# Attention of the second layer: two tiles of the second sequence's probabilities turned by squares instead of on TensorE, its bias added by GpSimd, and maxima ahead of value sums

## The chip, the cores and the metric

The kernel runs on one core of a Trainium2 chip. The core has five instruction queues that run beside each other and meet through semaphores: TensorE (PE: matmuls and 128x128 transposes, from SBUF into PSUM), VectorE (DVE), ScalarE (ACT), GpSimd (POOL) and SyncE (SP, which here only issues transfers). Transfers (DMAs) that SP, ACT and POOL issue are carried out by 16 DMA engines. The metric is the time of one execution on the device in microseconds; smaller is better. The kernel before takes 454.44 us (median of 3 runs, 454.12 to 454.5).

## The reference, cut to what matters

Two sequences (b = 0, 1) of 512 rows with 512 numbers, in float32, go through two layers: an attention with a memory matrix and a feed-forward net with ternary weights, then a plain attention and a feed-forward net, a layer norm after each of the four. The change is in the third of these, the plain attention with one head of 128:

```
qkv = einsum('bsc,cf->bsf', x, Wqkv) + bqkv          # 512 -> 3 x 128
q, k, v = qkv[:, :, 0], qkv[:, :, 1], qkv[:, :, 2]   # after a reshape
attn = softmax(einsum('bqd,bkd->bqk', q, k) / sqrt(128))
out = einsum('bqk,bkd->bqd', attn, v)
x = layernorm(x + einsum('bqd,dc->bqc', out, Wo) + bo)
```

After it comes `x = layernorm(x + (silu(x @ Wg.T) * (x @ Wu.T)) @ Wd.T)`, which is where the kernel spends its last 180 us.

## The kernel before, in words

All names below are of the kernel; line numbers are those of the profile. P is 128, a tile is 128 rows of 512 numbers, NT = 4 tiles make a sequence (t = 0 to 3), NK = 4 blocks of 128 columns make a row, TURNED = 2, SQ = 32.

**Order of the work.** The program is written in one order; a scheduler puts the instructions of each engine in a fixed order of its own, except on POOL, whose order is that of the text. `tc.issue_after(x.ins)` tells it that what follows in the block comes after x. An engine runs its queue strictly in order, so an instruction that waits holds up all behind it. PSUM has eight banks of 128x512, handed out by `psum(name)`; who takes a bank waits until the last reader of what stood in it is done.

**Turning a matrix.** A matmul contracts over partitions, so rows have to be transposed. The kernel does it in two ways. (1) TensorE transposes blocks of 128x128 into PSUM with the identity, and ScalarE or VectorE copies the result to SBUF: `transposed` (L118 to L131) does so for a whole sequence, block by block, four transposes from four tiles and a copy per block. (2) By squares: VectorE's `transpose` turns each 32x32 square of a tile where it stands (L1195), and `move_squares` (L301) moves the 4x4 kinds of squares to their places by transfers of 32 partitions each; `queues=3` gives SP eight of them, POOL four, and VectorE copies the four on the diagonal (L320); `queues=2` gives SP eight and POOL eight; `queues=1` gives SP twelve, with the diagonal.

**The stage.** For each sequence b (loop at L1147), TensorE makes q and k (`pqk`, L1163; ScalarE adds their bias, L1169) and v for each tile (`pv`, L1181), and VectorE adds the bias of v, reading PSUM (L1187). Sequence 0 then goes on at once: `scores` (L1110) makes four tiles of q k (`psc`, L1117), each in its own bank; `maxima` (L1120) takes the largest of each row on VectorE (L1123) and scales it (L1124); `exponentials` (L1129) lets ScalarE write the probabilities and their sums (L1139). The probabilities of sequence 0 are turned by squares (L1195 and, in the second pass of the loop, `move_squares(squares, pt0)`), while GpSimd adds the output bias bo to its rows (L1196). In between, `split_up` prepares the next feed-forward weights: ScalarE takes the upper part of a weight (L1033), VectorE forms two remainders (L1043 reads a part and the weight, L1044 two parts; all in SBUF).

For sequence 1: four score tiles, four maxima, four exponentials, then a table load on ScalarE for the later Silu (L1096). A small copy on POOL, `landed` (L1209), waits until the squares of sequence 0 have landed; behind it POOL issues four transfers that add bo from memory to the rows of sequence 1 (L1211). `split_up(2)` follows the maxima.

Then the ends of both sequences, in TensorE's order: `values(0, pt0, 1)` (L1228: probabilities times v, four matmuls into one bank, copied to `ot` by ScalarE, L1233), the 16 transposes of the probabilities of sequence 1 (`transposed`, L128, two copies on VectorE and two on ScalarE, L130), the four output products of sequence 0 (`output`, L1245), `values(1, pt1, 2)` in two halves of the query rows (tiles 0 and 1, then 2 and 3; each half copied to `ot` by VectorE), three output products of sequence 1, 16 transposes of the finished rows of sequence 0 for the feed-forward net (`turn_rows`, L1295), the fourth output product, and the feed-forward products (L1398, L1353). Beside it, `attended` (L1250) adds a product, divided by the sum of the exponentials, to the rows on VectorE; `norm_a1` takes statistics on VectorE (L138, L140), three short steps on POOL (L146, L147, L1240) and the norm itself on ScalarE (L1241).

Of the kernel before, what the change touches and what calls it, by code (L numbers as in the profile page):

```python
# [10 lines left out]
F32 = mybir.dt.float32  # L11
# [8 lines left out]
P = 128  # L20
# [10 lines left out]
SQ = 32  # L31
# [8 lines left out]
def kernel(  # L40
# [285 lines left out]
    def pair_tile(name, dtype=F32):  # L326
        return wop.tile([P, 2, HID], dtype, tag="wo", name=name)
# [764 lines left out]
    def table(func, behind):  # L1092

        with tc.issue_after(behind.ins):
            warm = small.tile([1, 1], F32, tag="warm", name=f"warm_{func.name}", bufs=1)
            nc.scalar.activation(warm, ln_eps[0:1], func)  # L1096
# [29 lines left out]

        return got, maxima

    def exponentials(b, got, behind={}):  # L1129
        sums = small.tile([P, NT], F32, tag="sums", name=f"sums_{b}")  # L1130
        row = []
        for t, (p, mx) in enumerate(got):
            if t % 2 == 0:
                two = pair_tile(f"prob_{b}_{t}")
            e = two[:, t % 2, :]
            with ExitStack() as tied:
                if t in behind:
                    tied.enter_context(tc.issue_after(behind[t].ins))
                moved = nc.scalar.activation(  # L1139
                    e, p, AF.Exp, bias=mx, scale=scale, accum_out=sums[:, t : t + 1]  # L1140
                )
            row.append(e)
        probs.append((row, sums))
        return moved

    qkv = []
    for b in range(B):  # L1147
        if b:
            with tc.issue_after(copies[-2].ins), tc.issue_after(copies[-1].ins):
                split_up(0, room0)  # L1150
                split_up(1, room1[:6])
        qk = []
        qk2 = query_tile(f"qk_{b}")
        if b == 0:
            v2 = query_tile("v")
        pqk = [psum(f"pqk_{b}_{j}") for j in range(2)]
        xt = [xt_a11[:, :TURNED], xt_a11[:, TURNED:]] if b else xt_a10
        for half in (1, 0) if b else (0, 1):
            for j in range(2):
                for k in range(NK):  # L1160
                    p = pqk[j].rearrange("p (h t i) -> p h t i", h=2, i=P)[:, half]
                    rows = xt[half][:, :, k, :]
                    nc.tensor.matmul(  # L1163
                        p, wqkv[:, k, ts(j, D)], rows,
                        start=(k == 0), stop=(k == NK - 1),
                    )
        for j, p in enumerate(pqk):
            s = qk2[:, j, :]
            moved = nc.scalar.activation(s, p, AF.Identity, bias=bqk[:, j : j + 1])  # L1169
            qk.append(s)  # L1170
        if b:
            pt0 = fp.tile([P, NT, NK, P], F32, tag="it10", name="pt_p0", bufs=1)
            move_squares(squares, pt0)
            pt0 = pt0.rearrange("p t k i -> p k t i")
        else:
            table(AF.Exp, moved)
        v = v2[:, b, :].rearrange("p (t d) -> p t d", t=NT)
        for t in range(NT):
            p = psum(f"pv_{b}_{t}")
            for k in range(NK):  # L1180
                nc.tensor.matmul(  # L1181
                    p[:, :D],
                    xt[t // TURNED][:, t % TURNED, k, :],
                    wqkv[:, k, ts(2, D)],
                    start=(k == 0), stop=(k == NK - 1),
                )
            nc.vector.tensor_add(v[:, t, :], bv, p[:, :D])  # L1187
        qkv.append((qk[0], qk[1], v))
        if b == 0:
            got, maxima = scores(0, turn_others)  # L1190
            maxima(range(NT))
            exponentials(0, got)
            squares = fp.tile([P, NT, HID], F32, tag="it00", name="squares_p0", bufs=1)
            for t in range(NT):
                nc.vector.transpose(squares[:, t, :], probs[0][0][t])  # L1195
                nc.gpsimd.tensor_add(xs[0][t], xs[0][t], bo)  # L1196
# [5 lines left out]
            weight_upper(gus[turn[2]][:, a].rearrange("p k i -> p (k i)"), room2[3 * a])  # L1202

    got, maxima = scores(1)
    scaled_max = maxima(range(NT))
    table(AF.Silu, exponentials(1, got))

    landed = small.tile([P, 1], F32, tag="off", name="landed")
    nc.gpsimd.tensor_copy(landed[2 * SQ : 3 * SQ], pt0[2 * SQ : 3 * SQ, NK - 1, NT - 1, P - 1 :])  # L1209
    for t in range(NT):  # L1210
        nc.gpsimd.dma_start(xs[1][t], bo_in.to_broadcast([P, HID]), accum_op=ALU.add)  # L1211
    with tc.issue_after(scaled_max.ins):
        done = split_up(2, room2, True)
    with tc.issue_after(done.ins):
# [6 lines left out]
    def values(b, pt, cuts):  # L1221

        ot = ot2[:, b, :]
        w = S // cuts
        for i in range(cuts):
            po = psum(f"pot_{b}_{i}")
            for k in range(NT):
                nc.tensor.matmul(  # L1228
                    po[:, :w].rearrange("p (t i) -> p t i", i=P), qkv[b][2][:, k, :],
                    pt[:, k, ts(i, NT // cuts)],  # L1230
                    start=(k == 0), stop=(k == NT - 1),
                )
            (nc.vector.tensor_copy if b else nc.scalar.copy)(ot[:, ts(i, w)], po[:, :w])  # L1233
        ots.append(ot)
# [8 lines left out]
    def output(b, t):  # L1243
        p = psum(f"po1_{b}_{t}")
        nc.tensor.matmul(p, ots[b][:, ts(t, P)], wo1, start=True, stop=True)  # L1245
        return p

    def attended(b, t, p):
        x = xs[b][t]
        return nc.vector.scalar_tensor_tensor(  # L1250
            x, p, probs[b][1][:, t : t + 1], x, ALU.mult, ALU.add
        )
# [46 lines left out]
        return pts, turned  # L1299

    values(0, pt0, 1)
    pt1 = transposed(probs[1][0], "p1").rearrange("p k (t i) -> p k t i", t=NT)
    for t in range(NT):
        attended(0, t, output(0, t))
        norm_a1(0, t)
    values(1, pt1, 2)
    for t in range(NT - 1):
        done = attended(1, t, output(1, t))
    rooms = [rows_room(0, "r0"), None]
    x3 = [row_blocks(rooms[0]), None]  # L1310
    pts, turned = turn_rows(0)
    with tc.issue_after(turned.ins):
        p = output(1, NT - 1)
    in_turn = Chain(done)
    for pt, (h, m, _) in zip(pts, x3[0]):
        in_turn(lambda: upper_lower(pt, h, m)[1])
    for t in range(NT - 1):
        in_turn(lambda: norm_a1(1, t))
    in_turn(lambda: attended(1, NT - 1, p))
    x = xs[1][NT - 1]  # L1320
    stats = layernorm_stats(x, f"a11_{NT - 1}")
    in_turn.last = taken[f"a11_{NT - 1}"]
    squares = xtp.tile([P, NT, HID], F32, tag="xt", name="squares_r1")
    for t in range(NT - 1):
        in_turn(lambda: nc.vector.transpose(squares[:, t, :], xs[1][t]))
    in_turn(lambda: layernorm_apply(x, x, stats))
    in_turn(lambda: nc.vector.transpose(squares[:, NT - 1, :], x))
    for h, m, d in x3[0]:
        in_turn(lambda: crossed(d, h, m))
    xt_r1 = fp.tile([P, NT, NK, P], F32, tag="it10", name="xt_f11", bufs=1)  # L1330
# [233 lines left out]
    for i, (b, j) in enumerate(steps):  # L1564
        held.append(up1(b, j, held))
        finished = held[0][0]
        if i == AHEAD:
            with tc.issue_after(in_turn.last.ins), tc.issue_after(uppers.ins):
                moved = finish_up()
        elif i > 1:  # L1570
            while len(held) > 1:
                moved = finish_up()
        if i == 1:
            in_turn(lambda: split_up(AHEAD - 1, take(6)))
        elif i == 2:
            rooms[1] = rows_room(1, "r1")
            x3[1] = row_blocks(rooms[1])
            for k in range(NK):
                with tc.issue_after(in_turn.last.ins):
                    uppers, in_turn.last = rows_from_squares(k)  # L1580

            landed = small.tile([P, 1], F32, tag="off", name="landed_r1")
            nc.gpsimd.tensor_copy(landed[:SQ], x3[1][NK - 1][0][:SQ, S - 1 :].bitcast(F32))
            gus[2:6] = up_weights(gu1_in, "1", range(2, 6), nc.gpsimd)
            wds = down_weights(wd1_in, "1", nc.gpsimd)
        elif i == AHEAD:
            for h, m, d in x3[1]:
                in_turn(lambda: crossed(d, h, m))
        with tc.issue_after(moved.ins):
            if ahead <= last and finished == 1:  # L1590
                split_up(
                    ahead, room0 if ahead == AHEAD else take(6 if turn[ahead] < last else 4)
                )
                ahead += 1
            for _ in range(2):
                if len(down_parts) <= last and len(free) >= (15 if ahead <= AHEAD + 3 else 9 if ahead <= last else 3):
                    split_down()
        if (b, j) == (1, last - 1):
            quarters = [split_tile(0, 0)]

        if i == last:

            with tc.issue_after(moved.ins):
                nc.gpsimd.drain()
# [69 lines left out]
```

## Time and profile before

| | |
|---|---|
| median of 3 runs | 454.44 us (454.12 to 454.5) |
| the profiled execution | 453.49 us, of which the span from the first to the last instruction is 451.7 us |
| mean granted clock of TensorE | 0.997 of full speed |
| TensorE busy | 445.1 us, 99% of the span, 1921 matmuls and transposes |
| VectorE, ScalarE, GpSimd busy | 318.2 (70%), 259.7 (57%), 127.6 us (28%) |
| stage 248 to 257 us | TensorE 9.00 us busy, VectorE 8.05, ScalarE 7.01, GpSimd 3.82 |
| stage 257 to 268 us | TensorE 11.00 us busy, VectorE 9.84, ScalarE 5.19, GpSimd 3.94 |

How to read the lines that follow. In a timeline line stand the start and the length in us from the span's start, the engine, the line of the kernel, the operation, what it writes and reads with the shapes, how many instructions are merged (x2), and in brackets how long the engine had been idle before and what ended the wait. The chain of waits goes back from the last instruction, at each step to what released it or to the instruction before it on its engine; it gives the share of each engine and, told in order of time, start, length, engine, name and line. Two instructions that follow each other on an engine overlap a little in the records (the next one starts before the end of the last is recorded), so the time that an operation takes from a queue is the distance of the starts. A float32 matmul with 512 columns is recorded as two passes of 0.43 us. PEld is TensorE's weight load, POOLq and SPq the queues' own work.

### The profile page before, as it was taken

Reading aid. Unit: us, or ns where it says so; the run is one execution under the profiler, and the core shown is the slowest. Engines: PE = TensorE matmul, PEld = TensorE weight load, DVE = VectorE, ACT = ScalarE, POOL = GpSimd, SP = SyncE. Lnnn points to the kernel's source line nnn. Section 1 sums busy time; section 2 is a strip of 40 time slices with the busy share of each in tenths; the row PEclk is TensorE's granted clock in tenths of the full one; section 3 lists DMA queues with packets and bytes.
Section 4 is the critical chain, followed back from the end, with each engine's and each line's share of the span. In section 5 each row is a group of like instructions: output and inputs, shape, how many; then the busy total and the mean of one; then the engine's idle time right before and its main releaser. Section 6 shows DMA issues by size and latency. Waiting matters only on the chain.

```text
span 451.7 us, 5899 instructions
## 1 busy us (share of the span) xinstructions
PE 445.1 (99%) x1921; PEld 339.8 (75%) x1921; DVE 318.2 (70%) x638; ACT 259.7 (57%) x494; POOL 127.6 (28%) x184
## 2 busy tenths in 40 slices
PE   8999999999999999999999999999999999999995
PEld 8887754344587888888878578888888888888885
DVE  3976658887886798858899999545535447777423
ACT  5787996567466975557745645454645446442311
POOL 0210306566650059202365337350000000011211
PEclk9999999999999999999999999999999999999998
DMA  7999990020028001132126603390000000000101
GB/s 271 364 284 312 193 336 26 0 36 14 1 49 267 10 2 48 48 94 41 32 35 159 101 1 55 89 386 2 0 1 0 0 3 0 1 23 23 48 23 70
DMA packets 37220, 38.97 MB, mean 86 GB/s; under 512 B 25264, under 2 KB 26160, under 8 KB 37184
## 3 DMA queue, kind: packets, MB, share of 16 engines
q1 hardware_dynamic: 32960, 26.66, 18.9%
q0 software_dynamic: 3936, 11.47, 10.9%
q8 instruction: 22, 0.36, 0.3%
q10 hardware_dynamic: 288, 0.36, 0.2%
q14 instruction: 14, 0.11, 0.1%
HBM read 32.45 MB, written 2.10 MB: 76 GB/s over the span
## 4 chain that ended last, share of the span: by engine, by line
PE 98%; ACT 0%; DVE 0%; issue 0%; DVEq 0%; ACTq 0%
PE pu L1353 24%; PE pd L1353 13%; PE po L593 12%; PE pq L538 9%; PE pg_f L789 9%; PE pu_f L789 9%; PE pd_f L848 4%; PE pqk L1163 3%; PE pu L1398 2%; PE pv L1181 2%; PE pot L1228 2%; PE psc L1117 2%; PE po L1245 2%; PE pmw L579 2%; PE pq L509 1%; PE rise L113 1%
## 5 line engine op out<-in xcount | busy, mean ns | idle before, releaser
L593 PE MATMUL po<-mw,q 128*128 128x512 f32 x128 | 56.6, 597 | 0.0
L146 POOL TENSOR_TENSOR rstd_f<-mv_f,ln_eps 128x1 f32<-128x1 f32 x15 | 5.4, 357 | 163.9 <-DVE mv_f L1521 128.8
L1353 PE MATMUL pu<-r,ugu 128*128 128x512 f32 x200 | 48.6, 389 | 0.0
L364 ACT ACTIVATE pu<-pu 128x512 f32<-128x512 f32 x42 | 24.3, 581 | 41.4 <-PE pu L1353 37.6
L593 PEld LDWEIGHTS po<-mw,q 128*128 128x128 f32 x128 | 23.1, 189 | 32.0 <-issue 18.0
L1353 PEld LDWEIGHTS pu<-r,ugu 128*128 128x128 f32 x200 | 37.6, 188 | 7.8
L615 DVE SCALAR_TENSOR_TENSOR x<-po,den,x 128x511 f32<-128x511 f32 x40 | 29.8, 745 | 2.1
L170 ACT ACTIVATE ta_f<-y_f,below_half 128x512 int8<-128x512 f32 (+1 forms) x22 | 15.9, 721 | 24.6 <-DVE y_f L158 22.2
L610 POOL TENSOR_TENSOR y<-y,y 128x511 f32<-128x511 f32 x16 | 21.8, 1360 | 22.0 <-ACT y L606 21.3
L1412 DVE TENSOR_TENSOR it_f<-ev,pu 128x512 f32<-128x512 f32 x20 | 13.7, 684 | 16.0 <-PE pu L1353 15.6
L1353 PE MATMUL pu<-r,it_early 128*128 128x512 f32 x104 | 24.9, 389 | 0.0
L1241 ACT ACTIVATE x<-x,off_f,rstd_f 128x512 f32<-128x512 f32 x7 | 5.7, 815 | 31.6 <-POOL off_f L1240 31.6
L815 DVE SCALAR_TENSOR_TENSOR it_f<-tb_f,ta_f 128x512 fp32r<-128x512 int16 (+1 forms) x22 | 15.6, 708 | 11.1 <-ACT tb_f L171 11.1
L1353 PEld LDWEIGHTS pu<-r,it_early 128*128 128x128 f32 x104 | 19.5, 188 | 4.1
L1353 PE MATMUL pd<-ugu,r 128*128 128x512 f32 (+1 forms) x79 | 22.5, 362 | 0.0
L789 PE MATMUL pg_f<-x,tu 128*128 128x512 f32 x88 | 22.1, 393 | 0.0
L789 PE MATMUL pu_f<-x,tu 128*128 128x512 f32 x88 | 21.7, 389 | 0.0
L376 POOL TENSOR_SCALAR td<-wd,inv_down 128x512 fp32r<-128x512 f32 x11 | 19.9, 1825 | 3.2 <-DVE inv_down L206 3.2
L597 ACT ACTIVATE den<-po,den_eps 128x1 f32<-128x1 f32 x64 | 14.3, 272 | 11.1 <-PE po L593 11.0
L848 PE MATMUL pd_f<-td,it_f 128*128 128x512 f32 x88 | 20.3, 389 | 0.0
L789 PEld LDWEIGHTS pg_f<-x,tu 128*128 128x128 f32 x88 | 16.4, 188 | 3.9 <-DVE x L615 0.4
L789 PEld LDWEIGHTS pu_f<-x,tu 128*128 128x128 f32 x88 | 16.5, 188 | 3.5
(400 smaller groups left out, 1131.4 us busy)
## 6 DMA issues: line engine op xcount, KB each, us to landing
gu<-in_gu SPq DMA_DIRECT2D x16, 512.0 KB, 4.6
wo<-in_wo SPq DMA_DIRECT2D x8, 512.0 KB, 9.1
wo<-in_wo POOLq DMA_DIRECT2D x8, 512.0 KB, 9.7
wd<-in_wd SPq DMA_DIRECT2D x10, 256.0 KB, 5.6
wd<-in_wd POOLq DMA_DIRECT2D x10, 256.0 KB, 6.5
wq<-in_wq SPq DMA_DIRECT2D x8, 256.0 KB, 5.3
gu<-in_gu POOLq DMA_DIRECT2D x4, 512.0 KB, 5.0
x<-in_x SPq DMA_DIRECT2D x7, 256.0 KB, 5.4
```

Of the source, the lines that this page charges most:

```text
L170: nc.scalar.activation(a[:n], y, AF.Relu, bias=below_half[:n])
L364: return nc.scalar.activation(p, p, AF.Copy, scale=BIG + 1.0)
L376: eng.tensor_scalar(out, w, factor, None, ALU.mult)
L538: done = nc.tensor.matmul(p, w, x, start=(start and i == 0), stop=(i == len(todo) - 1), skip_group_check=not start,)
L593: nc.tensor.matmul(po, qs[b][h0 + j][:, ts(t, P)], mw[:, h0 + j, :], start=True, stop=True,)
L597: nc.scalar.activation(den[:, j : j + 1], po[:, LAST:], AF.Identity, bias=den_eps)
L610: nc.gpsimd.tensor_add(ys[0][:, :LAST], ys[0][:, :LAST], y[:, :LAST])
L615: steps.append(nc.vector.scalar_tensor_tensor(x[:, :LAST], four[j][:, :LAST], d, x[:, :LAST], ALU.mult, ALU.add))
L789: nc.tensor.matmul(pp[a], t[:, a, i % NK, :], x2[b][i], start=(i == 0), stop=(i == 2 * NK - 1),)
L815: nc.vector.scalar_tensor_tensor(it[:n], tb[:n], 128.0, ta[:n], ALU.min, ALU.subtract)
L848: nc.tensor.matmul(pd, inter[b][c][:, ts(t, P)], td[c].bitcast(F32R), start=(c == 0), stop=(c == last),)
L1353: done = nc.tensor.matmul(p, w, x, start=(start and i == 0), stop=(i == n - 1), skip_group_check=not start,)
```

## The change

Of the four tiles of sequence 1's probabilities, tiles 0 and 1 are turned by squares (VectorE's transposes L1217, then 16 transfers, eight from SP and eight from POOL) and tiles 2 and 3 by TensorE, tile by tile (`pt_p1_2` copied by ScalarE, `pt_p1_3` by VectorE, L1321). The maxima of tiles 0 and 1 are put ahead of the sums of the values, one of these sums comes behind them, and the rest behind the last maximum; each turned tile's transpose stands ahead of the maximum two tiles later. The output bias of sequence 1 is added by four sums on GpSimd (L1224) in the place of `landed` and the four transfers. `values` takes its halves from the last to the first, and the outputs of sequence 1 follow as tiles 2, 3, 0 and, last, 1. The table load for Silu comes behind the copy of the first tile that TensorE turned, and the fourth weight's split (`split_up(AHEAD - 1)`) is told to come after that copy. In the program that comes out, the first value product of sequence 0 (`pot_0_0`) gets the PSUM bank of the first score tile of sequence 1 (`psc_1_0`); before, it got that of the first value tile (`pv_1_0`).

```diff
-    def exponentials(b, got, behind={}):
-        sums = small.tile([P, NT], F32, tag="sums", name=f"sums_{b}")
-        row = []
-        for t, (p, mx) in enumerate(got):
...
+    def exponentials(b, got, tiles=range(NT)):
+        if 0 in tiles:
+            pairs = [pair_tile(f"prob_{b}_{t}") for t in range(0, NT, 2)]
+            sums = small.tile([P, NT], F32, tag="sums", name=f"sums_{b}")
+            probs.append(([u for two in pairs for u in units(two)], sums))
+        row, sums = probs[b]
+        for t in tiles:
+            p, mx = got[t]
+            moved = nc.scalar.activation(
+                row[t], p, AF.Exp, bias=mx, scale=scale, accum_out=sums[:, t : t + 1]
+            )
         return moved
+
+    values_read = []
+
+    def add_values(tiles):
+        for _ in tiles:
+            v, p = values_read.pop(0)
+            nc.vector.tensor_add(v, bv, p)
...
-            nc.vector.tensor_add(v[:, t, :], bv, p[:, :D])
+            values_read.append((v[:, t, :], p[:, :D]))
         qkv.append((qk[0], qk[1], v))
         if b == 0:
+            add_values(range(NT))
...
     got, maxima = scores(1)
-    scaled_max = maxima(range(NT))
-    table(AF.Silu, exponentials(1, got))
-
-    landed = small.tile([P, 1], F32, tag="off", name="landed")
-    nc.gpsimd.tensor_copy(landed[2 * SQ : 3 * SQ], pt0[2 * SQ : 3 * SQ, NK - 1, NT - 1, P - 1 :])
+    squares1 = fp.tile([P, NT, HID], F32, tag="it00", name="squares_p1", bufs=1)
+    pt1 = xtp.tile([P, NT, NK, P], F32, tag="xt", name="xt_p1")
+
+    scaled_max = maxima(range(TURNED))
+    with tc.issue_after(scaled_max.ins):
+        add_values([0])
+    exponentials(1, got, range(TURNED))
+    for t in range(TURNED):
+        turned = nc.vector.transpose(squares1[:, t, :], probs[1][0][t])
+        with tc.issue_after(turned.ins):
+            scaled_max = maxima([TURNED + t])
+        exponentials(1, got, [TURNED + t])
+    with tc.issue_after(turned.ins):
+        add_values(range(1, NT))
     for t in range(NT):
-        nc.gpsimd.dma_start(xs[1][t], bo_in.to_broadcast([P, HID]), accum_op=ALU.add)
+        nc.gpsimd.tensor_add(xs[1][t], xs[1][t], bo)
+    move_squares(squares1[:, :TURNED], pt1[:, :TURNED], queues=2)
     with tc.issue_after(scaled_max.ins):
         done = split_up(2, room2, True)
...
-        for i in range(cuts):
+        for i in reversed(range(cuts)):
             po = psum(f"pot_{b}_{i}")
...
     values(0, pt0, 1)
-    pt1 = transposed(probs[1][0], "p1").rearrange("p k (t i) -> p k t i", t=NT)
+    for t in range(TURNED, NT):
+        pt = psum(f"pt_p1_{t}")
+        for k in range(NK):
+            nc.tensor.transpose(pt[:, ts(k, P)], probs[1][0][t][:, ts(k, P)], ident)
+        move = nc.vector.tensor_copy if t % 2 else nc.scalar.copy
+        moved = move(pt1[:, t], pt.rearrange("p (k i) -> p k i", k=NK))
+        if t % 2 == 0:
+            table(AF.Silu, moved)
+            settled = moved
+    pt1 = pt1.rearrange("p t k i -> p k t i")
     for t in range(NT):
         attended(0, t, output(0, t))
         norm_a1(0, t)
     values(1, pt1, 2)
-    for t in range(NT - 1):
+
+    *others, final = [*range(TURNED, NT), *range(TURNED)]
+    for t in others:
         done = attended(1, t, output(1, t))
...
-        p = output(1, NT - 1)
+        p = output(1, final)
...
         if i == 1:
-            in_turn(lambda: split_up(AHEAD - 1, take(6)))
+            with tc.issue_after(settled.ins):
+                in_turn(lambda: split_up(AHEAD - 1, take(6)))
```

The places left out rename `NT - 1` to `final` and `range(NT - 1)` to `others` in the steps of sequence 1 that follow.

More of the change, by code (lines that the diff above doesn't have):

```diff
@@ L1127, in scores @@
         return got, maxima
-    def exponentials(b, got, behind={}):
-        sums = small.tile([P, NT], F32, tag="sums", name=f"sums_{b}")
-        row = []
-        for t, (p, mx) in enumerate(got):
[L1133 to L1143, printed above, removed]
-        return moved
+    def exponentials(b, got, tiles=range(NT)):
[9 more added lines that the diff above has]
+            )
+        return moved
+    values_read = []
[3 more added lines that the diff above has]
+            nc.vector.tensor_add(v, bv, p)
     qkv = []
@@ L1316 @@
         in_turn(lambda: upper_lower(pt, h, m)[1])
-    for t in range(NT - 1):
+    for t in others:
         in_turn(lambda: norm_a1(1, t))
[L1319 to L1322, printed above, removed]
+    in_turn(lambda: attended(1, final, p))
+    x = xs[1][final]
+    stats = layernorm_stats(x, f"a11_{final}")
+    in_turn.last = taken[f"a11_{final}"]
     squares = xtp.tile([P, NT, HID], F32, tag="xt", name="squares_r1")
-    for t in range(NT - 1):
+    for t in others:
         in_turn(lambda: nc.vector.transpose(squares[:, t, :], xs[1][t]))
     in_turn(lambda: layernorm_apply(x, x, stats))
-    in_turn(lambda: nc.vector.transpose(squares[:, NT - 1, :], x))
+    in_turn(lambda: nc.vector.transpose(squares[:, final, :], x))
     for h, m, d in x3[0]:
```

## The prediction

> **What bounds the kernel now.** I read the page's chain of work first, then the timeline of the attention stage of the second layer (245 to 268 us), then what GpSimd's sums do to VectorE elsewhere. The chain says that TensorE is the bound from end to end, and that the transposes which the change halves lie on it (they are the 1.75 us of L128 in the chain told in order of time):
>
> ```profile
> PE 98%; ACT 0%; DVE 0%; issue 0%; DVEq 0%; ACTq 0%
> ...
> 254.41 1.75 PE pt_p L128 x16
> ```
>
> So time leaves only if TensorE's queue gets shorter and nothing else is late. The timeline by engine shows what could be late. VectorE, from its copies of the first sequence's squares to its first product's sum:
>
> ```profile
> 246.91 1.28 DVE L320 COPY pt_p<-squares_p 32x512 f32<-32x512 f32 x3
> 248.22 0.88 DVE L1187 TENSOR_TENSOR v<-bv,pv 128x128 f32<-128x128 f32 x4
> 249.02 0.68 DVE L1123 TENSOR_REDUCE mx<-psc 128x1 f32<-128x512 f32 x1
> ...
> 255.32 0.69 DVE L130 COPY xt_p<-pt_p 128x512 f32<-128x512 f32 x1 [0.49 <-PE pt_p L128]
> 256.20 0.69 DVE L130 COPY xt_p<-pt_p 128x512 f32<-128x512 f32 x1 [0.18 <-PE pt_p L128]
> 257.12 0.75 DVE L1250 SCALAR_TENSOR_TENSOR x<-po,sums,x 128x512 f32<-128x512 f32 x1 [0.23 <-PE po L1245]
> ...
> 261.90 0.39 DVE L1233 COPY ot<-pot 128x256 f32<-128x256 f32 x1
> ```
>
> The reader is to see that VectorE idles for 0.49 + 0.18 + 0.23 = 0.90 us in these 9 us and is otherwise full: it is nearly a second bound. TensorE at 262.89 starts the second sequence's output products, whose first operand is the copy that ends at 262.29: 0.6 us of slack.
>
> Third, what a GpSimd sum does to VectorE:
>
> ```profile
> 74.56 1.27 POOL L622 TENSOR_TENSOR x<-x,y 128x511 f32<-128x511 f32 x1 [2.32 <-DVE den L601]
> 75.94 3.24 POOL L610 TENSOR_TENSOR y<-y,y 128x511 f32<-128x511 f32 x2
> ...
> 75.27 1.11 DVE L211 SCALAR_TENSOR_TENSOR junk<-tu,sc_up,gu 128x512 int8<-128x512 f32 x1
> ...
> 76.42 1.63 DVE L211 SCALAR_TENSOR_TENSOR junk<-tu,sc_up,gu 128x512 int8<-128x512 f32 x1
> ...
> L290 DVE TENSOR_TENSOR x<-xt_f,x x4: 382/416/1491, 111.0 to 113.5; 128x256 fp32r<-128x256 f32 x4
> ...
> 239.34 1.27 POOL L1196 TENSOR_TENSOR x<-x,bo 128x512 f32<-128x512 f32 x1
> ...
> 240.07 1.09 DVE L1043 SCALAR_TENSOR_TENSOR it_early<-it_early,gu 128x512 fp32r<-128x512 f32 x1
> ```
>
> L211, L290 and L1043 read two tensors from SBUF. Alone they take 0.75, 0.42 and 0.68 us (the L290 line is that of the source view: shortest, median and longest ns); beside a sum of GpSimd they end about one operation after the sum's own end. Operations that read PSUM or one tensor keep their time beside the sums: the maxima 0.68, the transposes 0.71.
>
> **The change, part by part.** All sums are against the profiled execution: 453.49 us, of which 451.7 are the span. The median of the runs is 454.44, 0.95 above it; differences are added to either.
>
> *TensorE's work.* Eight of the 16 transposes go: 8 x 1.75/16 = 0.87 us. All else that it does keeps its count; this 0.87 is the most that the change can gain.
>
> *VectorE's work.* Two transposes are added, 0.64 us each from start to start (L1195, two in 1.29), and one of two copies of transposed tiles goes (0.69): +0.6 us. The four sums of the values and the maxima change places at no cost in work. Before, 257.12 - 248.22 less 0.90 idle is 8.0 us of work. After: 8.0 + 0.6, plus about 0.2 until the first score tile is there (the scores start at 247.38, two passes of 0.43 and 0.16 of drain: 248.4), plus about 0.3 in which a transpose waits for its exponential. So the first product's sum starts at 248.22 + 9.1 = 257.35, where TensorE, 0.87 earlier, has the product at 256.2. VectorE now sets the pace: from here to the copy of L1233 takes 262.29 - 257.12 = 5.2 us, a copy more of delay for the next stage: 262.6 to 262.7 against TensorE's want at 262.89 - 0.87 = 262.0. TensorE idles for 0.7, and of the 0.87 there remain 0.15. This part alone: 453.35.
>
> *GpSimd's sums.* Four of them (4.97 us for the four at L1196, 1.235 apart) stand right behind its last transfer issue for the first sequence, which ends at 245.24; the landed copy, which held the queue until 249.33, is gone, and nothing else holds them. So they run from 245.26, when VectorE has exactly its operations of the other kind: L1043, L1044 with two tensors in SBUF and the four copies of L320, until 248.19. The trace of before has no such meeting of these copies with a sum; the bounds are rows. From below: nothing, if VectorE keeps its turn and the sums wait (111.01: a sum took 1.84 us, since two operations of L290, close behind each other, went first). From above: a sum holds up one operation each time, by the longest row 1.49 - 0.415 = 1.08 us (the second L290 at 113.5): 4 x 1.08 = 4.3 us. What decides is whether GpSimd gets in between two VectorE operations. The three last copies do not overlap the operation before them in the trace (246.91, 247.34, 247.77, each 13 ns after the end of the last), and in 75.94 to 77.5 the engines took turns over a gap of 44 ns. So three hold-ups I take as likely, a fourth (the L1044 at 246.22) as an even chance; each costs between 1.63 - 0.75 = 0.88 and 1.08, 0.98 in the mean: 2.9 to 3.9 us until the copies are done, at 251.1 to 252.1 instead of 248.19.
>
> *Where that delay goes.* The first maximum then starts 2.7 to 3.7 us after its 248.4. The exponential ends 1.7 us later (0.72 + 0.15 + 0.78 + handing over), at 252.8 to 253.8. The first value product of sequence 0 (L1228, at 250.82) now takes the PSUM bank of the first score tile, so it waits for that exponential: a new wait, with 0.7 us of slack if nothing is held up, and TensorE idles 2 to 3 us in front of it. Behind that, the VectorE chain worked out above shifts by the same delay, and TensorE meets it at the output products. With its 0.15 kept and 0.2 of the shift absorbed by the wait for the scores: +2.4 to +3.5, middle +3.0.
>
> *Transfers.* 16 transfers of half the size replace nothing on these queues until 276.5 (SP) and 259.5 (GpSimd's first root). Eight on SP are 0.66 apart and land about 1.9 after their issue (xt_a: 231.21 to 237.67); eight on GpSimd are 0.64 apart. From the second transpose's end at about 252.7 the last lands at 259.3 to 260; the products' second half, which reads them, comes at 260.3, since the change puts the half of the TensorE-turned tiles first. With the hold-up both shift by about the same. Margin 0.3 to 1. The far row is 16 transfers of twice the size, 8.7 us from first issue to last landing (276.55 to 285.26): then 1.1 us late. I take 0, by the nearer row, and keep 1.1.
>
> *At nothing:* the four accumulating transfers that go (the last landed at 259.16, read at 263.95) and the table load, which moves behind a copy into 257 to 260.7, where ScalarE idles 3.7 us; without that cover it would cost its 1.28 us. GpSimd's root of the first norm stands behind the eight issues, which end at 258.2, needed at 259.4. The step tied to the settled table runs at 296 in a queue that had idled 3 us.
>
> The Trainium skill, "SBUF - State Buffer", section "Who interferes with whom", speaks against this change: a VectorE operation with two SBUF inputs, or in a two-port mode (copies), and a GpSimd operation that reads SBUF exclude each other for the whole instruction, and who issues first goes first. By it each hold-up would cost up to a whole sum, 1.27 us, four of them 5.1, about +4.7 in the end; the rows above show somewhat less (1.08 at most), and they decide.
>
> **Rivals.**
> A, forecast: the sums hold up the copies three or four times. 453.49 + 3.0 = 456.5 in the profile, 457.4 as a median; its own range 456.4 to 458.2. For it: six rows with hold-ups; against: none with these copies.
> B, not slower: GpSimd waits instead. Its sums then end at 253.2, just before the transfers need its queue. What is left is -0.15: 454.3. For it: the 1.84 us of L622. It decides if the first maximum starts before 248.65; up to 249.5 (one hold-up) the sum still gives only +0.85, 455.3.
> C: VectorE's extra work is hidden, the 0.87 is kept: 453.6. For it: nothing but that my 0.3 for waits could be too much; against: VectorE's 0.90 us of idle time.
> D: as A, but the transfers land 1.1 late as well: 458.5.
>
> **How the numbers follow.** About 0.2% (0.9 us) is what a measurement of this kernel can tell from no change. Chances: A 0.58, B 0.25 (of which 0.1 with one or two hold-ups), C 0.07, D 0.10. The predicted time is A's, 457.4. B and C together are too likely to leave out, so the range begins at B's 454.2; it ends at 458.5 with D. C and tails lie outside. Faster by over 0.2% would need more than the whole 0.87: 0.09, for C with an error in its base. Same: most of B, 0.22. Slower: A, D and the hold-ups of B that cost more than the middle, 0.69.
>
> **What would show it.** A right: L320's copies after 246.9 at 1.2 to 1.5 us instead of 0.42, the first maximum at 251 or later, TensorE idle in front of the first L1242 (pot) with the exponential as releaser. B right: copies at 0.42, GpSimd's sums of up to 4 us, the maximum at 248.4, and TensorE idle in front of the second sequence's output products, waiting for the copy of ot. D: TensorE waits for a transfer in front of the second half. I am wrong if GpSimd's sums start later than 245.3, or if VectorE's chain is shorter than 8.6 us.

## The result, and the profile after

The changed kernel takes 459.75 us (median of 6 runs, 458.68 to 460.52) against 454.28 us of the kernel before (6 runs, 453.71 to 454.5): a ratio of 1.0126, 95% interval 1.0111 to 1.0142. It is 5.5 us slower; the prediction was 3.0 us slower (457.4 against 454.44), and the measured time lies above its range, which ended at 458.5. The profiled execution took 460.27 us, with a span of 458.5 us.

The timeline of VectorE in the changed kernel, from its last splits ahead of the copies of the squares to its first maximum (start, length, engine, line, operation):

```profile
244.46 6.66 DVE L1044 TENSOR_TENSOR it_early<-it_early 128x512 fp32r<-128x512 f32 x2
...
252.67 1.28 DVE L320 COPY pt_p<-squares_p 32x512 f32<-32x512 f32 x3
253.98 0.69 DVE L1123 TENSOR_REDUCE mx<-psc 128x1 f32<-128x512 f32 x1
```

The two L1044 are 0.68 us long when alone. The first starts at 244.46 and keeps that time. The second starts at 245.07 and ends at 251.12: 6.06 us for a 0.68 us operation. This operation is none of those that the prediction named: it stands in front of the L1043 with which they begin. The copies of L320 behind it, which the prediction saw being held up one by one, keep their 0.42 us each. What happened in these 6 us stands in the timeline of GpSimd:

```profile
245.64 4.92 POOL L1224 TENSOR_TENSOR x<-x,bo 128x512 f32<-128x512 f32 x4
258.29 4.60 POOL L316 DMA_DIRECT2D xt_p<-squares_p  x8 [7.73 <-DVE mx L1124]
```

The four sums take 4.92 us, no longer than the four undisturbed ones of sequence 0; they end at 250.56, and the held operation ends 0.56 us later. GpSimd's whole run of sums went ahead of one VectorE operation. The timeline of TensorE shows what it cost:

```profile
247.77 3.60 PE L1117 MATMUL psc<-qk 128*128 128x512 f32 x8
255.72 6.28 PE L1242 MATMUL pot<-pt_p,v 128*128 128x512 f32 x8 [4.35 <-ACT prob L1137]
```

TensorE idles 4.35 us in front of the first value product, released by the exponential, as the prediction named it. But then the eight passes of this product take 6.28 us, where the same eight took 3.60 us before. The stretches of 1 us say why (busy time of PE, its weight loads, DVE, ACT and POOL, then the granted clock of TensorE, the DMA share and GB/s):

```profile
253.00:254.00 1.00, 0.00 (x0) 0.00 (x0) 0.94 (x4) 0.00 (x0) 0.00 (x0) 1.00 0.00 0
254.00:255.00 1.00, 0.00 (x0) 0.00 (x0) 0.97 (x3) 0.10 (x1) 0.00 (x0) 0.56 0.00 0
...
257.00:258.00 1.00, 1.00 (x2) 0.41 (x2) 1.00 (x4) 0.00 (x0) 0.00 (x0) 0.50 0.05 16
...
260.00:261.00 1.00, 1.00 (x3) 0.35 (x2) 1.00 (x3) 0.00 (x0) 1.00 (x3) 0.53 0.62 117
```

TensorE's work ended at 251.4; from about 254.1 to 261 its clock is granted at half. The prediction had no such term.

So three things have to be told apart: what the change does without the sums, what the sums do to VectorE, and what the idle time does to TensorE's clock. Executions differ by some tenths of a microsecond ahead of this stage, so stages are compared by two distances inside one profiled execution: from the first score matmul (psc) to the first maximum, and from the first score matmul to the first feed-forward product (pu, the work that follows the stage). They are taken from the starts of the instructions.

| kernel | psc to first maximum | TensorE idle ahead of pot | psc to pu | median us | ratio to before |
|---|---|---|---|---|---|
| before | 1.64 (value sums first) | 0 | 20.29 | 454.28 | 1 |
| changed | 6.21 | 4.35 | 26.68 | 459.75 | 1.0126 (1.0111 to 1.0142) |
| no_sums | 1.06 | 0 | 19.98 | 453.70 | 0.9990 (0.9981 to 0.9999) |
| before_sums | 7.03 | 2.97 | 26.49 | 459.03 | 1.0108 (1.0092 to 1.0123) |
| apart | 5.86 | 4.00 | 26.69 | 460.16 | 1.0140 (1.0124 to 1.0155) |
| filled | 6.23 | 0.50 | 25.13 | 459.12 | 1.0120 (1.0105 to 1.0135) |
| two | 3.78 | 1.93 | 22.63 | 456.73 | 1.0061 (1.0045 to 1.0078) |
| gated | 1.06 | 0 | 19.99 | 453.51 | 0.9988 (0.9978 to 0.9999) |
| best | 1.06 | 0 | 19.57 | 453.13 | 0.9987 (0.9976 to 0.9998) |

The kernel before took 454.28 us beside the changed kernel, 454.11 us beside no_sums, before_sums, apart and filled, and 453.93 us beside two, gated and best (medians). Each ratio is against the runs beside which its kernel ran; it is worked out from the single runs and is not the quotient of two medians.

### The profile page after: what moved, and what is told of

Its sections match the earlier page's. It is cut to its first block, busy times and chain, and to the rows that moved or that the text cites. A ratio compares the mean times of both kernels' runs of the same rounds, so it can differ in the third digit from the quotient of the medians.

```text
span 458.5 us, 5907 instructions
## 1 busy us (share of the span) xinstructions
PE 447.3 (98%) x1913; PEld 339.1 (74%) x1913; DVE 324.0 (71%) x639; ACT 259.1 (57%) x493; POOL 134.1 (29%) x191
## 4 chain that ended last, share of the span: by engine, by line
PE 87%; DVE 8%; ACT 3%; DMA 1%; issue 1%; POOL 0%; ACTq 0%; DVEq 0%; POOLq 0%
PE pu L1378 23%; PE pd L1378 13%; PE pg_f L789 9%; PE pq L538 9%; PE pu_f L789 9%; PE po L593 8%; PE pd_f L848 4%; PE pot L1242 2%; DVE it_early L1044 2%; PE pu L1423 2%; PE po L1259 2%; DMA gu<-in_gu 1%; DVE x L615 1%; PE pmw L579 1%; PE pq L509 1%; PE rise L113 1%
## 5 line engine op out<-in xcount | busy, mean ns | idle before, releaser
L146 POOL TENSOR_TENSOR rstd_f<-mv_f,ln_eps 128x1 f32<-128x1 f32 x15 | 6.4, 429 | 163.1 <-DVE mv_f L1546 128.0
L848 PEld LDWEIGHTS pd_f<-td,it_f 128*128 128x128 f32 x88 | 16.5, 188 | 3.4
```

The lines of the kernel that those rows point to most:

```text
L848: nc.tensor.matmul(pd, inter[b][c][:, ts(t, P)], td[c].bitcast(F32R), start=(c == 0), stop=(c == last),)
```

## The experiments

**no_sums: the change without GpSimd's sums.**

```diff
-    for t in range(NT):
-        nc.gpsimd.tensor_add(xs[1][t], xs[1][t], bo)
     move_squares(squares1[:, :TURNED], pt1[:, :TURNED], queues=2)
```

> The changed kernel without the four sums of GpSimd: the output bias is not added to the rows of sequence 1, all else stands in the same order. Theory (the loss is the four sums' hold on VectorE, and half speed of TensorE after its idle time): no L1044 of 6 us, the first maximum of sequence 1 at 248.4 to 248.6 instead of 253.98, TensorE idle for under 1 us in front of the first pot, granted clock 0.996 or more; the time is the before's less 0.15, 454.1 (453.7 to 454.7). Rival (the new PSUM bank of pot, the turned tiles' transfers or the moved table load cost by themselves): 455.5 or more.

Measured: 453.70 us beside 454.11 us, 0.4 us faster. Timeline of VectorE, then of TensorE:

```profile
247.65 1.28 DVE L320 COPY pt_p<-squares_p 32x512 f32<-32x512 f32 x3
249.19 0.69 DVE L1123 TENSOR_REDUCE mx<-psc 128x1 f32<-128x512 f32 x1 [0.26 <-PE psc L1117]
...
257.61 0.74 DVE L1262 SCALAR_TENSOR_TENSOR x<-po,sums,x 128x512 f32<-128x512 f32 x1
```

```profile
251.56 3.60 PE L1240 MATMUL pot<-pt_p,v 128*128 128x512 f32 x8
255.00 1.04 PE L1317 MATMUL pt_p<-ident,prob 128*128 128x128 f32 x8
...
262.82 2.83 PE L1257 MATMUL po<-wo,ot 128*128 128x512 f32 x6
...
266.18 1.64 PE L1307 MATMUL pt_f<-ident,x 128*128 128x128 f32 x13 [0.20 <-ACT x L1253]
```

The first maximum waits only for its scores (in this execution all of the stage lies 0.75 us later than in the one of before, so 249.19 is the forecast's 248.4), and the first value product comes without idle time. So neither the new PSUM bank, nor the transfers, nor the moved table load makes a loss: all of it comes with the sums. The rows also show where the gain goes: the second sequence's output products (po at 262.82) come 14.69 us behind the first scores, against 15.51 before, 0.82 of the 0.87 us; at the transposes of the finished rows of sequence 0 (pt_f), TensorE waits for the norm of a row (0.20 us are recorded as idle), and at pu 0.31 us are left.

**before_sums: only the sums, in the kernel before.**

```diff
-    landed = small.tile([P, 1], F32, tag="off", name="landed")
-    nc.gpsimd.tensor_copy(landed[2 * SQ : 3 * SQ], pt0[2 * SQ : 3 * SQ, NK - 1, NT - 1, P - 1 :])
     for t in range(NT):
-        nc.gpsimd.dma_start(xs[1][t], bo_in.to_broadcast([P, HID]), accum_op=ALU.add)
+        nc.gpsimd.tensor_add(xs[1][t], xs[1][t], bo)
```

> The kernel before with only one part of the change: GpSimd's four sums in the place of the landed copy and the four accumulating transfers. Theory: one VectorE operation that starts at about 245.3 (L1043) is held until all four sums are over, near 250.2, and lasts 5 to 6 us; the copies of the diagonal squares and the sums of the values end about 5.1 later, TensorE idles 3 to 3.5 us in front of the first pot, and the time is 457.7 to 459.8. Rival (the sums cost only together with the squares and the new order): 454.0 to 454.8. Rival of the record (each sum holds up one operation by 0.9 to 1.1): no operation over 2 us, 456.5 to 457.5.

Measured: 459.03 us beside 454.11 us, 4.9 us slower. Timelines of VectorE, GpSimd and TensorE:

```profile
244.68 6.67 DVE L1044 TENSOR_TENSOR it_early<-it_early 128x512 fp32r<-128x512 f32 x2
...
245.85 4.93 POOL L1209 TENSOR_TENSOR x<-x,bo 128x512 f32<-128x512 f32 x4
...
254.56 6.66 PE L1226 MATMUL pot<-pt_p,v 128*128 128x512 f32 x8 [2.97 <-DVE v L1187]
```

The same L1044 is held in the same way, with none of the squares, halves or maxima of the change. TensorE idles 2.97 us, this time for the value sums, and again works at half speed, as the granted clock (the third number from the end) shows: it falls in the first of these stretches of 1 us, comes back in the second, and is 0.50 in all between them:

```profile
253.00:254.00 1.00, 0.00 (x0) 0.00 (x0) 0.97 (x3) 0.00 (x0) 0.00 (x0) 0.86 0.00 0
...
260.00:261.00 1.00, 1.00 (x3) 0.32 (x2) 0.81 (x4) 0.99 (x3) 0.00 (x0) 0.73 0.00 0
```

This part alone makes nearly all of the loss: the stage is 6.20 us longer than before, in the changed kernel 6.39. The order of the maxima and the value sums changes what the first value product waits for and how long it waits (2.97 us instead of 4.35), but in either order it waits for VectorE.

**apart: the sums kept from following each other closely.** A copy of one column of each finished sum stands between the sums; it waits until the sum is written.

```diff
     for t in range(NT):
         nc.gpsimd.tensor_add(xs[1][t], xs[1][t], bo)
+        if t < NT - 1:
+            nc.gpsimd.tensor_copy(pause, xs[1][t][:, HID - 1 :])
```

> The changed kernel with a copy of one column out of each finished sum on GpSimd between the sums, which must wait for the sum before it; so the sums no longer overlap each other in GpSimd's pipeline. Theory (GpSimd keeps the port only because the next sum starts before the last one ends): VectorE gets in after every sum, so three or four different operations are held up by about 1 us each, none lasts over 2.5 us, the first maximum starts at 251.5 to 252.5, TensorE idles 1.8 to 3 us, 456.3 to 457.8. Rival (GpSimd goes first whenever it has something to do): one operation of 6 us or more again, first maximum at 254.0 to 254.6, 459 to 460.5.

Measured: 460.16 us. The time lies in the rival's range, but the operations are those of the theory. Two sizes of the theory were missed as well: the first maximum starts at 253.42 (expected 251.5 to 252.5), and TensorE idles 4.00 us (expected 1.8 to 3). Timelines of VectorE and GpSimd:

```profile
244.26 3.02 DVE L1044 TENSOR_TENSOR it_early<-it_early 128x512 fp32r<-128x512 f32 x2
247.19 0.68 DVE L1043 SCALAR_TENSOR_TENSOR it_early<-it_early,gu 128x512 fp32r<-128x512 f32 x1
247.80 1.48 DVE L320 COPY pt_p<-squares_p 32x512 f32<-32x512 f32 x1
...
249.88 3.51 DVE L320 COPY pt_p<-squares_p 32x512 f32<-32x512 f32 x3
...
245.43 1.28 POOL L1225 TENSOR_TENSOR x<-x,bo 128x512 f32<-128x512 f32 x1
...
247.28 1.72 POOL L1225 TENSOR_TENSOR x<-x,bo 128x512 f32<-128x512 f32 x1
```

Now four different operations are held: the second L1044 lasts 2.41 us instead of 0.68, and three copies of L320 last 1.48, 1.53 and 1.52 us instead of 0.41 to 0.42. That is the picture that the prediction had drawn, and the part of the theory about taking turns holds: with a gap between the sums VectorE gets in, and GpSimd waits too (1.72 us for the second sum instead of 1.28). But it saves nothing: 1.73 + 1.07 + 1.11 + 1.11 = 5.0 us of holds against 5.4 us in one piece. VectorE has more operations of the sensitive kind left (seven, from L1044 to the last copy) than there are sums, so every sum finds one to hold. What matters here is the time that the two engines need together, not how they take turns.

**filled: TensorE kept busy while it waits.**

```diff
+    room = values_read[-1][2]
+    for _ in range(6):
+        nc.tensor.matmul(room[:, D:], ident, wqkv[:, 0], start=True, stop=True)
```

(VectorE's order of work is kept as it was.)

> The changed kernel with six matmuls of 384 columns behind the scores on TensorE (3.9 us, their result is written to the unused part of a PSUM bank and never read), so that TensorE hardly idles while it waits for the exponential. Theory (part of the loss is TensorE at half speed after 2.8 us without work): the hold of VectorE and the first maximum at 254 stay, the granted clock is 0.996 or more in every execution, the first eight passes of pot take 3.5 us instead of 6.28, and the time is 458.5 to 458.8, 1.0 to 1.2 below the changed kernel's median of 459.75. Rival (the spread of the changed kernel's times has another cause): clock 0.989 in about half of the executions, 459.2 to 460.5.

Measured: 459.12 us (458.44 to 459.5); the profiled execution took 458.44 us, with a span of 456.6 us and a mean clock of 0.999. Timelines of VectorE and TensorE:

```profile
244.12 6.67 DVE L1044 TENSOR_TENSOR it_early<-it_early 128x512 fp32r<-128x512 f32 x2
...
250.86 4.03 PE L1215 MATMUL pv<-wqkv,ident 128*128 128x384 f32 x12
255.40 3.70 PE L1246 MATMUL pot<-pt_p,v 128*128 128x512 f32 x8 [0.50 <-ACT prob L1137]
```

VectorE is held exactly as in the changed kernel, but the value product takes 3.70 us instead of 6.28, and from the first scores to pu it takes 25.13 us instead of 26.68. So the half clock costs 1.55 us of the profiled execution, 1.1 less than the 2.7 by which the eight passes are longer; at least part of the difference is time in which TensorE would have waited for VectorE later on (0.62 us for the copy of ot in this kernel). The granted clock was 0.998 to 1.000 in all four executions of filled, as expected, and not 0.989 in half of them, as the rival had it. In the medians the gain is not resolved: 459.12 us is 0.6 below the changed kernel's 459.75, which had its runs at another time, the intervals of the ratios overlap, and the expected 458.5 to 458.8 was missed. The changed kernel's own six executions, each with its clock on record, point the same way: two with a mean clock of 0.995 and 0.996 took 458.68 and 458.77 us, four with 0.989 or 0.990 took 459.23 to 460.52. By an estimate from the traces, 6.8 us at half speed (last section) take 0.007 off the mean of a span of 458 us, so 0.995 and 0.996 leave no room for the whole of it: the half clock does not come to its full size in every execution.

**two: half of the sums.**

```diff
-    for t in range(NT):
+    for t in range(2):
         nc.gpsimd.tensor_add(xs[1][t], xs[1][t], bo)
```

> The changed kernel with two of the four sums of GpSimd: the output bias is not added to tiles 2 and 3 of sequence 1. Theory (the hold is the whole length of the run of sums, 1.22 us for each; TensorE falls to half speed only after 2.75 to 3 us without work, as the earlier runs' rows have it): one L1044 of 3.6 us instead of 6.06, the first maximum 3.8 us behind the first scores instead of 6.2, TensorE idle for 1.9 us in front of the first pot, no slice at half speed, and 456.7 (456.2 to 457.2). Rival (any such idle time brings the half speed): the same hold, the first eight passes of pot 6.3 us instead of 3.6, 458.0 to 458.6. Rival of the record (0.9 to 1.1 for each sum): 455.5 to 456.0.

Measured: 456.73 us (455.66 to 457.3), beside 453.93. Timelines of VectorE, GpSimd and TensorE:

```profile
243.87 4.23 DVE L1044 TENSOR_TENSOR it_early<-it_early 128x512 fp32r<-128x512 f32 x2
...
245.04 2.50 POOL L1224 TENSOR_TENSOR x<-x,bo 128x512 f32<-128x512 f32 x2
...
252.71 3.70 PE L1242 MATMUL pot<-pt_p,v 128*128 128x512 f32 x8 [1.93 <-ACT prob L1137]
```

The hold falls by the length of two sums: the second L1044 lasts 3.63 us, the first maximum comes 3.78 us behind the first scores (expected: 3.8), and TensorE idles 1.93 us and then runs at full speed (clock 0.999 in the profiled execution, 455.66 us). The median is the expected one, but by way of a sum that was 0.4 too high: from the stage's own distance, 22.63 - 20.29 = 2.3 us above 453.93 would be 456.3. The profiled execution is the fastest of the six; of the others, three had a mean clock of 0.998 to 1.000 and two had 0.993 (456.98 and 457.07 us), below the 0.997 to 1.000 of the kernel before in the runs beside them. So the rival is refuted for the profiled execution, but in two of six TensorE did lose clock. That it was the half clock in this stage is likely (0.007 is what its 6.8 us take off the mean) but not shown, since these two have no trace; and the times do not set them apart (the slowest, 457.30 us, had 0.998). The "2.75 to 3 us without work" of the theory was also not what the earlier rows say: in before_sums the half clock begins 2.1 us after TensorE's last work (last section).

**gated: all four sums, but later.** A copy of one column waits for the last copy of a diagonal square; the sums stand behind it.

```diff
+    landed = small.tile([P, 1], F32, tag="off", name="landed")
+    nc.gpsimd.tensor_copy(landed[3 * SQ :], pt0[3 * SQ :, NK - 1, NT - 1, P - 1 :])
     for t in range(NT):
         nc.gpsimd.tensor_add(xs[1][t], xs[1][t], bo)
```

> The changed kernel with a copy of one column on GpSimd ahead of its four sums that waits for the last copy of a diagonal square on VectorE, so the sums run beside VectorE's maxima, value sums and transposes instead of beside its splits and copies. Theory (only operations with two inputs in SBUF, and such copies, exclude GpSimd's sums): maxima 0.69, value sums 0.28 and transposes 0.65 to 0.71 as without the sums, the first maximum 1.1 to 1.6 us behind the first scores, GpSimd's transfers about 0.5 us later, which nothing waits for, full clock, and 453.7 (453.3 to 454.3), the time of the kernel without the sums. Rival (the sums hold up every VectorE operation that touches SBUF): transposes of 1.2 us and more, transfers 1 to 3 us later, 454.8 to 457.

Measured: 453.51 us, ratio 0.9988 (0.9978 to 0.9999). Timelines of GpSimd and VectorE:

```profile
248.94 4.94 POOL L1226 TENSOR_TENSOR x<-x,bo 128x512 f32<-128x512 f32 x4
253.81 4.59 POOL L316 DMA_DIRECT2D xt_p<-squares_p  x8
...
248.79 0.69 DVE L1123 TENSOR_REDUCE mx<-psc 128x1 f32<-128x512 f32 x1 [0.26 <-PE psc L1117]
...
250.98 0.71 DVE L1217 STREAM_TRANSPOSE squares_p<-prob 128x512 f32<-128x512 f32 x1 [0.25 <-issue]
252.19 0.69 DVE L1217 STREAM_TRANSPOSE squares_p<-prob 128x512 f32<-128x512 f32 x1
```

The same 4.94 us of sums now lie beside maxima, value sums and transposes, and none of them is as much as 0.01 us longer than in no_sums. The stage's distances in the table are those of no_sums within 0.01 us. So the loss comes from the meeting of the sums with operations that read two tensors in SBUF or copy within SBUF, and not from the sums as such. GpSimd's eight transfers are issued 0.65 us later, measured from the first scores, and the last of the 16 lands at 259.70, 1.0 us before the products' second half reads them (260.70).

**best: gated, and VectorE's copy of a turned tile given to ScalarE.**

```diff
-        move = nc.vector.tensor_copy if t % 2 else nc.scalar.copy
-        moved = move(pt1[:, t], pt.rearrange("p (k i) -> p k i", k=NK))
-        if t % 2 == 0:
-            table(AF.Silu, moved)
-            settled = moved
+        settled = nc.scalar.copy(pt1[:, t], pt.rearrange("p (k i) -> p k i", k=NK))
+    table(AF.Silu, settled)
```

> The gated kernel, and the second of the two tiles that TensorE turned is copied by ScalarE instead of VectorE; the table load follows this copy. Theory (what is left of the gain of 0.87 us without the sums, 0.31, is set by VectorE's chain through the norms of sequence 0; the copy takes 0.6 us of it): TensorE no longer idles in front of the transposes of the finished rows of sequence 0, and the time is 0.4 to 0.6 below the gated kernel, 453.2 (452.8 to 453.6), below both kernels. Rival (the rest of the gain goes in another place, or ScalarE's later table load costs as much): 453.6 to 454.3, no difference from the gated kernel.

Measured: 453.13 us, ratio 0.9987 (0.9976 to 0.9998). Timelines of VectorE, ScalarE and TensorE:

```profile
256.62 0.75 DVE L1266 SCALAR_TENSOR_TENSOR x<-po,sums,x 128x512 f32<-128x512 f32 x1
...
255.11 1.08 ACT L1322 COPY xt_p<-pt_p 128x512 f32<-128x512 f32 x2
...
264.83 2.00 PE L1311 MATMUL pt_f<-ident,x 128*128 128x128 f32 x16
```

VectorE's first product's sum comes 9.07 us behind the first scores instead of 9.48, the idle 0.20 us in front of the transposes of the finished rows is gone, and the stage is 0.42 us shorter than the gated one, 0.72 of the possible 0.87 shorter than before. Both gated and best beat the kernel before, by little: their intervals end just below 1. That best beats gated is shown by the profiled stages, not by the medians.

## Why the prediction was wrong, point by point

- **TensorE's 0.87 us.** Right: the transposes and the start of the output products behind them lie 0.87 us apart in no_sums (255.00 to 255.87), 1.75 before (254.25 to 256.00).
- **VectorE's added work gives most of it back.** The mechanism was right; the place and the size were off. The prediction had 0.7 us given back in front of the second sequence's output products. In no_sums these come in time (the copy of ot ends at 262.76, they start at 262.82); the gain is given back one step later, where TensorE waits for the norms of sequence 0, which hang on the same VectorE chain. 0.31 us are left in the profile and 0.4 us in the medians, instead of 0.15. The term mis-sized is the chain of 8.6 us and 0.3 of waits: from the first maximum to the first product's sum it took 8.42 us with its wait. A chain "shorter than 8.6 us" was one of the prediction's own signs of being wrong; it came, in no_sums, though it moved the time by under 0.2 us.
- **GpSimd's sums. This step failed.** The place and the time of the meeting were right: the sums start 2.13 us ahead of the first scores, forecast 2.12 (245.64 and 245.26 on their own scales). The operation was not: the sums held the L1044 that had begun 0.57 us before them, which the prediction left out, and not the L1043, L1044 and copies behind it. Nor were the count and the price right: "three hold-ups I take as likely" and a fourth "as an even chance" made 3.5 holds; "0.98 in the mean" for each made 3.4 us. The runs showed 5.4 us in one piece (changed, before_sums, filled), or 5.0 us in four pieces where the sums were kept apart: about the whole length of the four sums was added to VectorE's time. Both rows behind the 0.98 had VectorE's operation begin when the sum was already under way (L211 at 76.42 beside a sum from 75.94, L290 at 113.51 beside one from 113.28), so that they priced the rest of a sum. The three later holds of apart, 1.07 to 1.11 us, are close to the higher of these rows (1.08); the first, 1.73, is not, and neither is the unbroken hold. And the count rested on a gap of 13 ns on VectorE's side, where the sums leave none on theirs: each of them starts 0.05 us before the last one ends (4.92 us for four of 1.27). The prediction knew such overlap only as something that protects VectorE (the L290 pair), not as something that protects GpSimd; apart, where the sums do not overlap and VectorE gets in, shows that it does.
- **The Trainium skill's rule.** "SBUF — State Buffer", section "Who interferes with whom", has the pair of ports locked for the whole instruction. The prediction named the estimate from it, 5.1 us of holds and about +4.7 us in the end, but let its rows decide. The measurement was nearer to the page: 5.0 to 5.4 us of holds, and 25.13 - 20.29 = 4.8 us in the end without the half clock. What the page says of operations with one SBUF input agrees with gated: transposes of 0.69 and 0.71 us beside the sums, as without them.
- **Where the delay goes.** Right: TensorE idle in front of pot with the exponential as releaser, and a price somewhat below the hold. Of the hold of 5.38 us the wait for the scores absorbs 0.23 (forecast 0.2), which leaves the 5.15 us (6.21 - 1.06) by which the first maximum is late; less the 0.31 of gain (forecast 0.15) the stage would be 4.84 us longer, and that is what filled has (25.13 - 20.29).
- **Missing: TensorE's clock.** The forecast's 2 to 3 us of idle time became 4.35, and the half clock that followed took another 1.55 us in the profiled execution. The Trainium skill's "TensorE: Matmul & The Clock Gate" (section "HAM oscillation — how this bites in real kernels") warns of idle gaps of more than about 3.4 us; here 4.35, 4.00 and 2.97 us, the last below the page's figure, brought the half clock; 1.93 and 0.50 did not in the profiled executions (for 1.93, two other executions leave it open). The longest idle time in the prediction was near enough to that limit to deserve a bound; it had none.
- **Transfers, bank, table load, removed transfers: at nothing.** Right: in no_sums the last of the 16 transfers lands at 259.78 and is read from 261.10 on; the exponential that frees the bank ends at 250.88, 0.68 us before the value product, where the prediction had 0.7 of slack; the table load lies in ScalarE's idle time. Rival D fell with it. C fell because 0.31 us of the 0.87 are left and not all, and B (GpSimd waits instead) was refuted by the sums' undisturbed 4.92 us.

Together, in the profiled stage: -0.31 for the change without the sums, +5.15 for the hold, +1.55 for the clock, 6.39 us. Against the forecast's 3.0 that is 1.8 us for the mis-sized hold and 1.55 for the missing clock. The remaining 0.4 of the 6.8 us between the two spans had arisen before the stage began (first scores at 247.77 instead of 247.38).

## What to carry to other kernels

When work moves to GpSimd, look at what VectorE does in the same microseconds: beside operations that read two SBUF tensors or copy within SBUF, the sums of GpSimd added about their whole length to VectorE's chain here (5.0 to 5.4 us for 4.9), however the two took turns; beside maxima, transposes and sums that read PSUM they added nothing. So place such sums by a wait on the last sensitive operation; here a copy of one column turned a loss of 5.5 us into a gain of 0.4. And where a forecast puts a few microseconds of idle time on TensorE, price its half clock as well, as an end of the range.

## What the runs showed that was not expected

- A run of GpSimd sums that follow each other closely was not interrupted: one VectorE operation waited for four of them (6.06 us), or for two (3.63 us). With a copy between the sums that waits for the sum ahead of it, VectorE got in each time: it ended the held operation and did one more undisturbed after the first and after the second sum, and ended the held one after the third.
- The first sum of a run costs about 0.45 us more than its own length: 5.38 us held for 4.92 us of sums, 2.95 for 2.50, and 1.73 for the first of the separated sums, where the others cost 1.07 to 1.11. The held operation had started 0.57 us before the first sum's recorded start and should have been nearly done. Whether the sum takes hold before its record begins, or GpSimd's records are late, was not settled.
- The half clock did not come at one fixed time after TensorE's last work. Worked out from the clocks of the slices, it began 2.1 us after it in before_sums (253.72, work ended at 251.59), 2.7 us in the changed kernel (254.12, 251.37) and 3.1 us in apart (254.30, 251.17). It lasted for 6.8 us in all three, 5.2 to 6.0 us of them under load.
